# Layer 1's cross-attention on one Trainium2 core: value products turned round, on column quarters, with the sums of the weights from a second such product

## The chip, the cores and the metric

The kernel runs on one core of one Trainium2 chip. The core has five engines that the text names as the profile does: TensorE (PE, with its loads of the stationary operand as PEld), VectorE (DVE), ScalarE (ACT), GpSimd (POOL) and SyncE (SP). TensorE writes its products to PSUM[...]; POOL does not touch PSUM here. The metric is the device time of one execution in microseconds, as the median of several runs.

## The reference

A decoder of two layers works on x of 2 x 1024 tokens with 256 features, with a context of 2 x 64 tokens. Each layer has self-attention, cross-attention to the context and a feed-forward part, each followed by a layer norm. All of it is float32. The part that the change concerns is layer 1's cross-attention, with 16 heads of 16 features over 64 keys:

```python
qh = (q @ wq.T).reshape(bs, sq, N_HEADS, D_K).transpose(0, 2, 1, 3)
kh = (k @ wk.T).reshape(bs, sk, N_HEADS, D_K).transpose(0, 2, 1, 3)
vh = (v @ wv.T).reshape(bs, sk, N_HEADS, D_K).transpose(0, 2, 1, 3)
z = jnp.einsum('bhqd,bhkd->bhqk', qh, kh) / math.sqrt(D_K)
z = jnp.where(mask[:, None, :, :], jnp.float32(-10000000000.0), z)
z = jax.nn.softmax(z, axis=-1)
z = jnp.einsum('bhqk,bhkd->bhqd', z, vh)
z = z.transpose(0, 2, 1, 3).reshape(bs, sq, D_MODEL)
return z @ wo.T
```

The result is added to x and normalised; x then goes to the quantised feed-forward part, which needs the largest absolute value over all tokens before it can start.

## The kernel before, in words

The kernel is written as stages, one for each part of each layer. Layer 1's cross-attention is `l1_xattn` (L1528); it follows `l1_attn` and precedes `l1_ffn`. The 2048 tokens are cut into NT = 16 tiles of 128 tokens, and four tiles make a group (NG = 4 groups of GT = 512 tokens). The small helper functions of `l1_xattn` each issue one step for one tile:

- `queries(g)` (L1552) makes the transposed queries of a group, two PSUM banks of 512 columns; one bank is copied out by DVE, one by ACT.
- `softmax(n)` makes the scores of all 16 heads for 128 tokens in two 512-column products (L1567, against a block-diagonal form of the keys, into the tile `wide`), copies those that the mask keeps over a tile set to -1e10 (DVE, L1571, onto POOL's memset of L1564), takes the maxima (DVE, L1576), subtracts them (POOL, L1577) and takes the exponential (ACT, L1578).
- `turn(n)` transposes the weights by pairs of heads, so that the 2 x 64 keys of a pair lie on the 128 partitions (eight transposes, L1588), and copies the two halves out of PSUM, one by ACT (L74 in `evac`) and one by DVE (L70).
- `mix(n)` multiplies: the turned weights are the stationary operand, and `vblk`, which holds the values of the pair's two heads, each with a column of ones, is the moving operand (L1603). The output has tokens on partitions, and for each head 16 sums of values and one sum of weights. DVE takes the reciprocals of the 16 sums of weights (L1608) and multiplies (L1610) into `lxtok`.
- `back(n)` transposes `lxtok` by two 128x128 transposes (L1620), and ACT copies the result to `lxtokT`.
- `output(n)` multiplies by the output weights (L1634), adds the residual on DVE (L1637), and, after the third and fourth tile of a group, normalises (`normalise`, L178 to L200, with a power on POOL at L183) and takes the largest absolute value (L1644).

`vblk` is filled earlier, in `prepare` (L1447 on), whose steps are issued during layer 0's feed-forward part.

The order of the work is set in two ways. TensorE's order is written out by hand: the loop at the end of `l1_xattn` stands in a `manual_schedule` for that engine, and issues in turn the scores two tiles ahead, this tile's transposes, the output of three tiles ago, the transposes back of two tiles ago and the products of one tile ago:

```python
for n in range(NT + 3):
    ...
    softmax(n + 2)
    if n < NT:
        turn(n)
    output(n - 3)
    back(n - 2)
    mix(n - 1)
```

The orders of VectorE, ScalarE and POOL within the stage are chosen when the kernel is built, by a scheduler[...]. PSUM is shared out as two tiles `wide` of two banks, three single banks (`bank`, used by queries, turn, back and output in turn) and one accumulator (`acc`, used by `mix` alone): the products of a tile can start only when DVE has read those of the tile before.

Of the kernel before, what the change touches and what calls it, by code (L numbers as in the profile page):

```python
# [9 lines left out]
F32 = mybir.dt.float32  # L10
# [5 lines left out]
ALU = mybir.AluOpType  # L16
AX = mybir.AxisListType

P = 128
B, S, D = 2, 1024, 256  # L20
# [13 lines left out]
class Decoder:  # L34
# [11 lines left out]
    def pool(self, name, bufs, **kw):  # L46

        return self.tc.tile_pool(name=name, bufs=bufs, reuse_waits="tile", **kw)
# [1339 lines left out]
    def prepare(self, tmp):  # L1388
        nc, t, late = self.nc, self.t, self.late
        H = 16  # L1390
# [14 lines left out]
        for name in ("wq", "wo", "wk", "wv"):  # L1405
            w = tmp.tile([P, 2, D], F32, tag="lxw", name="lxw")
            nc.sync.dma_start(w, t["L1_xattn_" + name].rearrange("(o p) d -> p o d", p=P))
            ps = self.bank()
            for d in range(2):
                for o in range(2):  # L1410
                    k = 2 * d + o
# [10 lines left out]
        ps = self.bank()  # L1422
        for m in range(2):
            for c in range(2):
                nc.tensor.matmul(
                    ps[:, m * P : (m + 1) * P], lhsT=wT["wk"][:, c, m * P : (m + 1) * P],
                    rhs=self.ctxT[:, c, :], start=c == 0, stop=c == 1,
# [11 lines left out]
        ps = self.bank()  # L1439
        for b in range(B):  # L1440
            for c in range(2):
                nc.tensor.matmul(
                    ps[:, b * D : (b + 1) * D],
                    lhsT=twice[:, c, b].rearrange("p a k -> p (a k)"), rhs=wT["wv"][:, c, :],
                    start=c == 0, stop=c == 1,
                )
        self.vblk = late.tile([P, B, 8, 2, 17], F32, name="vblk")  # L1447
        nc.gpsimd.memset(self.vblk, 0.0)
        for k in range(2):
            rows = slice(k * SK, (k + 1) * SK)  # L1450
            nc.gpsimd.memset(self.vblk[rows, :, :, k, 16:17], 1.0)
            for b in range(B):
                nc.vector.tensor_copy(
                    self.vblk[rows, b, :, k, 0:16],
                    ps[rows, b * D : (b + 1) * D].rearrange("p (m k i) -> p m k i", k=2, i=16)[:, :, k, :],
                )
        yield
# [22 lines left out]
        for name in ("w_gate", "w_up"):  # L1480
            w = self.weight(None, NI, D)
# [16 lines left out]
        w = self.weight(None, 2, self.I)  # L1498
# [8 lines left out]
        for c in range(NI):  # L1507
            n = P if c < NI - 1 else last
# [6 lines left out]
        ps = self.bank()  # L1515
# [12 lines left out]
    def l1_xattn(self):  # L1528
        nc = self.nc
        H, NT = 16, T // P  # L1530
# [10 lines left out]
        with ExitStack() as s:  # L1541
            pool = lambda n, k: s.enter_context(self.pool(n, k))
            qp, pp, ptp, op = pool("lxq", 2), pool("lxp", 4), pool("lxpT", 3), pool("lxo", 3)
            qT, prob, turned, tok, tokT, res, new = {}, {}, {}, {}, {}, {}, {}
            wide = [P, H, SK]

            def queries(g):
# [33 lines left out]
            def turn(n):  # L1581
                p = prob.pop(n)
                turned[n] = ptp.tile([P, 8, P], F32, tag="lxpT", name="lxpT")
                for half in range(2):
                    ps = self.bank()
                    for k in range(4):
                        m = half * 4 + k
                        nc.tensor.transpose(  # L1588
                            ps[:, k * P : (k + 1) * P],
                            p[:, 2 * m : 2 * m + 2, :].rearrange("p h k -> p (h k)"), self.ident,  # L1590
                        )
                    self.evac(
                        turned[n][:, half * 4 : half * 4 + 4, :], ps.rearrange("p (k q) -> p k q", q=P),
                        by=nc.vector if half else nc.scalar,
                    )

            def mix(n):

                if not 0 <= n < NT:
                    return  # L1600
                ps = self.acc()[:, 0 : H * 17].rearrange("p (h i) -> p h i", i=17)
                for m in range(8):
                    nc.tensor.matmul(  # L1603
                        ps[:, 2 * m : 2 * m + 2, :], lhsT=turned[n][:, m, :],
                        rhs=self.vblk[:, n // 8, m].rearrange("p a i -> p (a i)"), start=True, stop=True,
                    )
                rz = self.sm.tile([P, H], F32, tag="lxrz", name="lxrz")
                nc.vector.reciprocal(rz, ps[:, :, 16])  # L1608
                tok[n] = op.tile([P, D], F32, tag="lxtok", name="lxtok")
                nc.vector.tensor_tensor(  # L1610
                    tok[n].rearrange("p (h i) -> p h i", i=16), ps[:, :, 0:16],
                    rz.unsqueeze(2).to_broadcast([P, H, 16]), ALU.mult,
                )

            def back(n):
                if not 0 <= n < NT:
                    return
                ps = self.bank()
                for c in range(2):
                    nc.tensor.transpose(  # L1620
                        ps[:, c * P : (c + 1) * P], tok[n][:, c * P : (c + 1) * P], self.ident
                    )
                tokT[n] = op.tile([P, 2, P], F32, tag="lxtokT", name="lxtokT")
                self.evac(tokT[n].rearrange("p c q -> p (c q)"), ps[:, 0:D], by=nc.scalar)

            def output(n):
                if not 0 <= n < NT:
                    return
                g, i = divmod(n, 4)
                if i == 0:  # L1630
                    res[g] = self.rp.tile([P, 4, D], F32, tag="r", name="r")
                ps = self.bank()[:, 0:D]
                for c in range(2):
                    nc.tensor.matmul(  # L1634
                        ps, lhsT=tokT[n][:, c, :], rhs=self.lxwoT[:, c, :], start=c == 0, stop=c == 1
                    )
                nc.vector.tensor_tensor(res[g][:, i, :], ps, self.x[g][:, i, :], ALU.add)  # L1637
                if i == 2:
                    new[g] = self.xp.tile([P, 4, D], F32, tag="x", name="xg")
                tiles = {2: range(3), 3: range(3, 4)}.get(i)  # L1640
                if tiles:
                    self.normalise(new[g], res[g], tiles)
                    k = 2 * g + i - 2
                    nc.vector.tensor_reduce(  # L1644
                        self.xm[:, k : k + 1], new[g][:, tiles.start : tiles.stop, :], AX.XY, ALU.max,
                        apply_absolute_value=True,
                    )
                if i == 3:
                    self.x[g] = new[g]

            with self.tc.manual_schedule(engines={mybir.EngineType.PE}):
                queries(0)
                softmax(0)
                softmax(1)
                for n in range(NT + 3):
                    if n < 4:
                        self.ends[n]()
                    if n % 4 == 1 and n // 4 + 1 < NG:
                        queries(n // 4 + 1)
                    softmax(n + 2)  # L1660
                    if n < NT:
                        turn(n)
                    output(n - 3)
                    back(n - 2)
                    mix(n - 1)


# [173 lines left out]
```

## Time and profile before

| What | Before |
|---|---|
| Median of 3 runs | 2464.19 us (2464.09 to 2467.39) |
| The profiled execution | 2464.71 us |
| Its span in the trace | 2462.9 us |
| PE busy over the span | 2331.8 us (95%) |
| DVE / ACT / POOL busy | 1677.5 / 1110.8 / 911.3 us |
| Layer 1's cross-attention, first scores to last maximum | 2254 to 2369.6 us |

The span is the time from the first to the last instruction of the program in the trace; the execution is 1.8 us longer. "Busy" is the time in which an engine has at least one instruction running. Matmuls overlap in the records, and their ends are modelled, so the start of one matmul to the start of the next tells more than the length of one. A float32 product or its weight load stands in the trace as two records. L numbers are lines of the kernel; L70 and L74 are the copies in the helper `evac`, and are told apart by the tile that they write. In a group's row the columns are: line, engine, operation, output and input with shapes, the count, then the busy time and the mean of one in ns, then the idle time before them with what ended it.

### The profile page before, as it was taken

What the parts mean: (1) busy time and instruction counts of PE and PEld (TensorE: products, weight loads), DVE (VectorE), ACT (ScalarE), POOL (GpSimd) and SP (SyncE); (2) the same over time, 40 slices, a digit from 0 to 9 for tenths busy, and PEclk for the clock granted to TensorE, in tenths of its full rate; (3) what the DMA queues carried; (4) which work ended last, traced back from release to release, by engine and by line L of the source; (5) the groups of instructions that cost most, each with busy time, mean ns of one, the idle gap of its engine ahead of it and who ended that gap; (6) DMA issues with size and microseconds to landing.
All of it is one profiled execution on the core that took longest, in us unless ns stands there. A gap on an engine that the chain in (4) does not pass through costs nothing. (4 is left out here: it accounts for less than half of the span.)

```text
span 2462.9 us, 37293 instructions
## 1 busy us (share of the span) xinstructions
PE 2331.8 (95%) x14062; PEld 1580.2 (64%) x14065; DVE 1677.5 (68%) x2916; ACT 1110.8 (45%) x1730; POOL 911.3 (37%) x747
## 2 busy tenths in 40 slices
PE   7999999999998999999999999999989999999974
PEld 3545545444545668899999999999734444444742
DVE  6888887888785334555555555545788687885786
ACT  4665565565563322233333333333156555664344
POOL 4666666566565222342343332332210001002412
PEclk9999999999999999999999999999999999999986
DMA  7888788688787001010010010100212121210001
GB/s 160 174 159 169 148 169 166 131 161 170 151 172 187 1 1 41 1 39 27 13 35 30 18 41 6 48 1 1 49 25 42 28 40 30 47 23 1 1 1 35
DMA packets 275667, 168.78 MB, mean 69 GB/s; under 512 B 47560, under 2 KB 262176, under 8 KB 275488
## 3 DMA queue, kind: packets, MB, share of 16 engines
q1 hardware_dynamic: 239072, 148.05, 28.6%
q10 hardware_dynamic: 36416, 18.36, 3.7%
q8 instruction: 111, 1.82, 0.3%
q14 instruction: 68, 0.56, 0.1%
HBM read 34.21 MB, written 2.10 MB: 15 GB/s over the span
## 5 line engine op out<-in xcount | busy, mean ns | idle before, releaser
L312 DVE TENSOR_REDUCE nm<-wide 128x1 f32<-128x1024 f32 x256 | 300.7, 1214 | 63.2 <-PE wide L297 62.3
L1186 DVE TENSOR_REDUCE most<-bank 128x1 f32<-128x512 f32 x476 | 300.4, 684 | 25.3 <-PE bank L1176 17.3
L1229 ACT ACTIVATE w<-wide 128x1024 f32<-128x1024 f32 x256 | 248.3, 1022 | 147.0 <-PE wide L1223 138.8
L297 PE MATMUL wide<-k,q 64*128 64x512 f32 x1024 | 271.5, 627 | 18.8 <-ACT p L317 17.4
L328 POOL TENSOR_SCALAR p<-p,sums 128x1024 f32<-128x1024 f32 x128 | 143.6, 1121 | 269.6 <-DVE sums L325 269.6
L379 PE MATMUL acc<-turned,v 128*64 128x256 f32 x2048 | 235.1, 382 | 2.2 <-ACT aoT L74 1.7
L379 PEld LDWEIGHTS acc<-turned,v 128*64 128x64 f32 x2048 | 142.6, 137 | 113.6 <-issue 30.7
L906 ACT ACTIVATE mhT<-mhT,cols 128x256 f32<-128x256 f32 (+1 forms) x256 | 143.3, 607 | 147.4 <-DVE mhT L934 105.0
L317 ACT ACTIVATE p<-wide,nm 128x1024 f32<-128x1024 f32 x128 | 142.8, 1116 | 144.9 <-DVE nm L312 118.2
L817 POOL TENSOR_TENSOR hs<-hs,mhT 128x1024 f32<-128x1024 f32 x31 | 102.5, 3307 | 241.6 <-DVE hs L815 241.6
L342 DVE STREAM_TRANSPOSE blocks<-p 128x1024 f32<-128x1024 f32 x128 | 158.0, 1234 | 43.0 <-DMA turned<-blocks 13.3
L297 PEld LDWEIGHTS wide<-k,q 64*128 64x128 f32 x1024 | 89.9, 187 | 146.1 <-issue 76.5
L183 POOL TENSOR_TENSOR rstd<-ve,nhalf 128x4 f32<-128x4 f32 (+2 forms) x28 | 26.1, 934 | 424.7 <-DVE ve L181 424.3
L917 PE MATMUL unit<-xT,w 128*128 128x256 f32 x768 | 182.3, 380 | 0.0
L974 DVE SCALAR_TENSOR_TENSOR r<-acc,gates,r 128x128 f32<-128x128 f32 x256 | 77.7, 345 | 140.4 <-PE acc L965 140.4
L342 DVE STREAM_TRANSPOSE blocks<-r 128x1024 f32<-128x1024 f32 x128 | 153.8, 1202 | 0.0
L917 PEld LDWEIGHTS unit<-xT,w 128*128 128x128 f32 x768 | 140.9, 190 | 16.9 <-issue 0.3
L328 POOL TENSOR_SCALAR r<-r,sums 128x1024 f32<-128x1024 f32 x128 | 143.6, 1122 | 0.0
L317 ACT ACTIVATE r<-wide,nm 128x1024 f32<-128x1024 f32 x128 | 142.2, 1111 | 1.1 <-DVE nm L312 0.9
L1243 PE MATMUL acc<-w,v 128*32 128x512 f32 x1024 | 137.2, 608 | 0.0
L1176 PE MATMUL bank<-kst,qst 64*128 64x512 f32 x476 | 125.9, 459 | 11.8 <-DVE most L1186 11.8
L362 POOL COPY turned<-blocks 32x1024 f32<-32x1024 f32 x128 | 132.0, 1031 | 4.0 <-DVE blocks L342 0.3
(333 smaller groups left out, 4479.3 us busy)
## 6 DMA issues: line engine op xcount, KB each, us to landing
turned<-blocks SPq DMA_DIRECT2D x636, 128.0 KB, 2.8
turned<-blocks ACTq DMA_DIRECT2D x132, 128.0 KB, 3.1
w<-in_L_ffn_W SPq DMA_DIRECT2D x16, 1024.0 KB, 5.3
q<-q SPq DMA_DIRECT2D x64, 128.0 KB, 2.3
k<-k SPq DMA_DIRECT2D x32, 128.0 KB, 2.6
qst<-qh SPq DMA_DIRECT2D x48, 64.0 KB, 2.4
qst<-ql SPq DMA_DIRECT2D x48, 64.0 KB, 2.4
kst<-kh SPq DMA_DIRECT2D x48, 64.0 KB
```

What stands on the lines that cost most here:

```text
L297: nc.tensor.matmul(sc[h][:, kb, :], lhsT=q[rows, qi, at : at + P], rhs=k[rows, ki, :], start=True, stop=True,)
L312: nc.vector.tensor_reduce(nm, sc, AX.XY, ALU.max, negate=True)
L317: nc.scalar.activation(p, sc.rearrange("p a c -> p (a c)"), AF.Exp, bias=nm, accum_out=sums[:, 0, h : h + 1],)
L328: nc.gpsimd.tensor_scalar(p, p, sums[:, 1, h : h + 1], 1.0, ALU.mult, ALU.mult)
L342: nc.vector.transpose(blocks[m][:, :, h, qt, :], p.rearrange("p (j q) -> p j q", q=32))
L362: nc.gpsimd.tensor_copy(b, a)
L379: nc.tensor.matmul(av[own[h], 0:256].rearrange("p (t i q) -> p i t q", t=2, i=4), lhsT=vals[u][:, kt, own[h]], rhs=p[:, h], start=kt == 0, ...
L906: nc.scalar.activation(hT[:, f, cols], hT[:, f, cols], AF.Relu, bias=self.cols[:, col : col + 1])
L917: nc.tensor.matmul(v[:, m, :], lhsT=up[e][k][:, f : f + P], rhs=self.halves[g][k], start=k in (1, 2, 5) and m == 0, stop=True, skip_group_ ...
L1186: nc.vector.tensor_reduce(most[n][:, kb, qt, h : h + 1], sc[a], AX.X, ALU.max, negate=True)
L1229: nc.scalar.activation(slot[:, k, :], ps[k].rearrange("p a q -> p (a q)"), AF.Exp, scale=0.25)
L1243: nc.tensor.matmul(mixed[n][o : o + 32, :], lhsT=vals[b][:, kt, 17 * h : 17 * h + 32], rhs=pT[:, a, :], start=kt == 0, stop=kt == 7, tile_ ...
```

## The change

The value product is turned round. The values become the stationary operand (32 columns: two heads of 16), and the turned weights (128 keys by 128 tokens) the moving one, so that the output has features on partitions and tokens along the free dimension. This is the form that `output` needs, so `back`, its two transposes and its copy are gone, and the loop has one step less in flight. Four pairs of heads go to four column quarters of the PE array (`tile_position=(0, 32 * j)`), that is to four groups of 32 partitions of the output. Two such sets of four make all 16 heads.

The sums of the weights can no longer be a 17th column of each head. They come from the same product with `vone` in place of `vblk`: ones for the keys of the one head in its 16 columns and for those of the other head in its 16. So every sum appears 16 times, once beside each feature, and the reciprocal is taken of a tile of 128 x 256 elements, where it was 128 x 16. Both copies of the turned weights are now made by ACT.

```diff
-        self.vblk = late.tile([P, B, 8, 2, 17], F32, name="vblk")
+        self.vblk = late.tile([P, B, 8, 2, 16], F32, name="vblk")
         nc.gpsimd.memset(self.vblk, 0.0)
+        self.vone = late.tile([P, 2, 16], F32, name="vone")
+        nc.gpsimd.memset(self.vone, 0.0)
         for k in range(2):
             rows = slice(k * SK, (k + 1) * SK)
-            nc.gpsimd.memset(self.vblk[rows, :, :, k, 16:17], 1.0)
+            nc.gpsimd.memset(self.vone[rows, k, :], 1.0)
             for b in range(B):
                 nc.vector.tensor_copy(
-                    self.vblk[rows, b, :, k, 0:16],
+                    self.vblk[rows, b, :, k, :],
...
                     self.evac(
                         turned[n][:, half * 4 : half * 4 + 4, :], ps.rearrange("p (k q) -> p k q", q=P),
-                        by=nc.vector if half else nc.scalar,
+                        by=nc.scalar,
                     )
...
-                ps = self.acc()[:, 0 : H * 17].rearrange("p (h i) -> p h i", i=17)
-                for m in range(8):
-                    nc.tensor.matmul(
-                        ps[:, 2 * m : 2 * m + 2, :], lhsT=turned[n][:, m, :],
-                        rhs=self.vblk[:, n // 8, m].rearrange("p a i -> p (a i)"), start=True, stop=True,
-                    )
-                rz = self.sm.tile([P, H], F32, tag="lxrz", name="lxrz")
-                nc.vector.reciprocal(rz, ps[:, :, 16])
-                tok[n] = op.tile([P, D], F32, tag="lxtok", name="lxtok")
-                nc.vector.tensor_tensor(
-                    tok[n].rearrange("p (h i) -> p h i", i=16), ps[:, :, 0:16],
-                    rz.unsqueeze(2).to_broadcast([P, H, 16]), ALU.mult,
-                )
-
-            def back(n):
-                if not 0 <= n < NT:
-                    return
-                ps = self.bank()
+                ps = self.acc().rearrange("p (a c q) -> p a c q", a=2, c=2)
                 for c in range(2):
-                    nc.tensor.transpose(
-                        ps[:, c * P : (c + 1) * P], tok[n][:, c * P : (c + 1) * P], self.ident
-                    )
+                    for a in range(2):
+                        for j in range(4):
+                            w = self.vone if a else self.vblk[:, n // 8, 4 * c + j]
+                            nc.tensor.matmul(
+                                ps[32 * j : 32 * j + 32, a, c, :], lhsT=w.rearrange("p a i -> p (a i)"),
+                                rhs=turned[n][:, 4 * c + j, :], start=True, stop=True,
+                                tile_position=(0, 32 * j),
+                            )
+                rz = op.tile([P, 2, P], F32, tag="lxrz", name="lxrz")
+                nc.vector.reciprocal(rz, ps[:, 1])
                 tokT[n] = op.tile([P, 2, P], F32, tag="lxtokT", name="lxtokT")
-                self.evac(tokT[n].rearrange("p c q -> p (c q)"), ps[:, 0:D], by=nc.scalar)
+                nc.vector.tensor_tensor(tokT[n], ps[:, 0], rz, ALU.mult)
...
-                for n in range(NT + 3):
+                for n in range(NT + 2):
...
-                    output(n - 3)
-                    back(n - 2)
+                    output(n - 2)
                     mix(n - 1)
```

More of the change, by code (lines that the diff above doesn't have):

```diff
@@ L1543, in l1_xattn @@
             qp, pp, ptp, op = pool("lxq", 2), pool("lxp", 4), pool("lxpT", 3), pool("lxo", 3)
-            qT, prob, turned, tok, tokT, res, new = {}, {}, {}, {}, {}, {}, {}
+            qT, prob, turned, tokT, res, new = {}, {}, {}, {}, {}, {}
             wide = [P, H, SK]
```

## The prediction

> **What bounds the kernel now.** First the page's busy times, then the table of stages, then the chain of waits inside the stage that changes.
>
> ```profile
> PE 2331.8 (95%) x14062; PEld 1580.2 (64%) x14065; DVE 1677.5 (68%) x2916; ACT 1110.8 (45%) x1730; POOL 911.3 (37%) x747
> ```
> TensorE (PE) has work throughout. The stage, layer 1's cross-attention, runs from about 2254 to 2369.6 us. The table of stages (length, then busy us of each engine, then the granted PE clock) for four of its tiles, and for the end from tile 12's value products:
> ```profile
> core 0: us, PE busy (x) PEld busy (x) DVE busy (x) ACT busy (x) POOL busy (x), PEclk, DMA share, GB/s
> 2289.87:2316.07 26.20, 25.81 (x146) 18.77 (x145) 19.90 (x40) 8.21 (x13) 12.73 (x11) 1.00 0.00 1
> 2347.92:2369.60 21.68, 15.05 (x108) 12.67 (x107) 15.98 (x49) 4.09 (x8) 4.97 (x8) 0.92 0.00 0
> ```
> Four tiles take 26.2 us, of which PE is busy 25.8 and VectorE (DVE) 19.9: DVE has 6.3 us to spare. The chain of waits through one tile lies wholly on PE:
> ```profile
> 2284.24 0.22 PE bank L1620 x2
> 2284.46 1.71 PE acc L1603 x16
> 2286.17 1.80 PE wide L1567 x4
> 2287.97 0.87 PE bank L1588 x8
> 2288.84 0.87 PE bank L1634 x4
> 2289.71 0.33 PE bank L1620 x2
> 2290.03 1.71 PE acc L1603 x16
> ```
> L1603 is the value product that is turned round, L1620 the transposes back that go. Single records step 0.1115 us, so sixteen occupy 1.78. The DVE group table gives the price of a reciprocal by row length (last field but one: mean ns):
> ```profile
> L620 DVE RECIPROCAL rs<-sum 128x4 f32<-128x4 f32 x4 | 0.7, 178 | 0.1
> L802 DVE RECIPROCAL esum<-esum 128x8 f32<-128x8 f32 x2 | 0.4, 203 | 0.1
> L1608 DVE RECIPROCAL lxrz<-acc 128x16 f32<-128x16 f32 x16 | 4.0, 251 | 4.2 <-PE acc L1603 4.2
> ```
> 178, 203, 251 ns at 4, 8, 16 elements: about 6.2 ns per element over 153 ns. And two views on the new product's kind, column quarters in layer 1's self-attention (timeline), and the clock (stages of 3.41 us):
> ```profile
> 2000.42 1.06 PE L1243 MATMUL acc<-w,v 128*32 128x512 f32 x8
> 2001.42 0.51 PE L1176 MATMUL bank<-kst,qst 64*128 64x512 f32 x2
> ```
> ```profile
> 2362.80:2366.22 3.42, 1.23 (x5) 0.68 (x4) 2.28 (x8) 0.37 (x1) 1.09 (x4) 1.00 0.00 0
> 2366.22:2369.63 3.41, 0.00 (x0) 0.00 (x0) 2.53 (x8) 0.00 (x0) 0.56 (x1) 0.50 0.00 0
> 2403.76:2407.18 3.42, 1.86 (x8) 0.77 (x8) 3.31 (x7) 2.06 (x3) 0.00 (x0) 1.00 0.00 0
> 2407.18:2410.59 3.41, 2.70 (x12) 1.11 (x11) 3.31 (x6) 1.38 (x2) 0.00 (x0) 1.00 0.00 0
> ```
> After a window in which PE was busy 1.23 us the clock is halved; after one with 1.86 us it is not.
>
> [...] four 512-column products in quarters end in 1.00 us until the next product, beside 0.86 for a single full-width one (1.72 for two at L1567). [...]
>
> **The change, part by part**, per tile of 128 tokens, 16 tiles.
> (1) Products: 8 of 1.78 us together become 16 in four rounds of four quarters. Each float32 product of 128 columns streams a quarter of 0.86 = 0.214 us; four rounds 0.86, [...] 0.14 after (1.00 - 0.86) and 0.10 before, by single records. I take 1.10. Bounds: 0.86 [...], 2.0 (weight loads of 106 ns not hidden in such short rounds), 3.4 (no overlap of quarters). PE gains 0.68.
> (2) The transposes back (0.22 on PE) and their copy on ScalarE (370 ns) go: PE gains 0.22. ScalarE has room (8.2 of 26.2 us busy), so this is worth 0.22 at most.
> (3) The second half of the weights' copy moves from DVE (680 ns, queue time 0.59) to ScalarE (0.58): two copies in a row there. The product that reads them is issued a whole tile later, which hides the second, so PE pays nothing; without that cover it would be 0.6 a tile. DVE's gain is counted in its sum below.
> (4) The reciprocal grows from 16 to 256 elements a partition: 153 + 256 x 6.25 = 1.75 us against 0.25; queue time 1.66 against 0.17. Bounds: 0.41 us, the rate of the division's multiply at L1610 (128x256, 407 ns)[...]. I take 1.75 since three rows lie on that line. The multiply keeps its size.
> (5) Setup: one more memset on POOL in the layer before (37% busy), no DMA moves, SP's queue is the same: nothing. If POOL were late there, tens of ns.
>
> PE per four tiles: 4 x (1.72 + 0.87 + 0.86 + 1.10) + 3.43 for the queries = 21.6 us instead of 25.2 (observed 26.2 with waits). DVE in queue time (start to start) per tile: masked copy 1.21, maximum 1.12, reciprocal 1.66, multiply 0.32, residual 0.33, statistics 0.39 = 5.03; per four with layer norm, maxima and a query copy (3.4) 23.5, where today's own sum gives 19.9. DVE also waits: twice for POOL's power (0.8 each in this trace) and about 0.8 on its own results: 25.9. **DVE becomes the bound, and the middle gains only 0.3 per four tiles, 1 us over twelve.** PE then waits: its output product needs the multiply, and in 6 of 16 tiles the issue order of the changed kernel puts a masked copy (1.21) between reciprocal and multiply. There product end to multiply end is 0.26 + 1.66 + 1.21 + 0.45 = 3.6 us, over PE's 2.6 us of scores and transposes; PE's queue stands behind the output product.
>
> The end, from tile 12's products: without scores to cover them, tiles run serially. Tile 12 to 13: DVE first works off layer norm, a maximum and a residual (about 5.9 us to tile 12's multiply), so 6.4; 13 to 14 and 14 to 15: 1.10 + 0.26 + 1.75 + 0.45 + 0.12 + 0.86 = 4.5, taken as 4.8 and 4.6 with the queue; tile 15 to the last maximum 8.6. Sum 24.4 against 21.7: +2.7.
>
> New: PE now idles 2 to 3.6 us at a time in this end (no gap over 0.7 us there today), so a clock window gets little work and the clock halves. On the path from tile 13 on: three products (0.85 more each) and four outputs (0.86 more each), 6.0 if all; I take 5.0.
>
> Sum: -1.0 + 2.7 + 5.0 = +6.7 on the profiled execution's 2464.71 (span 2462.9 and 1.8 around it), which is 0.5 above the median 2464.19. Rounded: **2470.5 us**.
>
> **Rivals.**
> The end keeps its clock (window edges fall well, or 1.2 us of products is enough): +1.7, 2466. For: the threshold lies somewhere from 1.23 to 1.86 us of work in a window. Against: one stall of 3.5 us fills a window.
> Faster: the reciprocal's price per element falls on long rows. Place: DVE between product and multiply. At 0.41 us DVE needs 18.2 us per four tiles, PE bounds again: up to 3 x (22.6 - 26.2) = -11, less the waits left, so -8: 2456. It decides below about 1.2 to 1.5 us. Against: the line through three row lengths; for: no row here is longer than 16.
> Dearer pieces: weight loads bare (2.0 us a tile)[...]: +9 to +17, 2477. For: rounds of 0.107 us are as long as a load's 106 ns. Against: quarters load beside each other, eight loads in 0.05 us at L1243.
> The quarters do not run side by side (the change does not do what it says): 16 x (3.4 - 1.1), PE the bound, about +33: 2497. Against: L1243.
>
> **Numbers.** Forecast 0.42, clock kept 0.25, cheaper reciprocal 0.15, dearer pieces 0.13, no overlap 0.05. A measurement tells 0.2%, 4.9 us, from no change. Slower: 0.39 of the forecast, 0.13, 0.05: 0.57. Same: most of "clock kept" and edges: 0.29. Faster: 0.14. The range 2459 to 2480 leaves out most of the cheap reciprocal (0.10), no overlap (0.05) and the dearest end (0.03). The likeliest case alone: 2468 to 2474.
>
> **What would show it.** Right: the reciprocal's row at 1.75 us x16; DVE busy near 23.5 of about 26 us per four tiles; PE idle before the output product, released by the multiply; a halved clock around the last four tiles; products near 1.1 us a tile. Wrong: a reciprocal well below 1.4 us, PE still without idle time, or products over 1.8 us.

## The result, and the profile after

The changed kernel takes 2476.76 us (median of 6 runs, 2473.67 to 2477.72); the kernel before takes 2467.39 us beside it (2464.09 to 2469.83). The ratio is 1.003, with a 95% interval of 1.0019 to 1.0041 (the two medians alone give 1.0038). Run again later beside another set of runs of before, the same two kernels gave 1.0018 (1.0009 to 1.0027). The change makes the kernel slower by 0.2 to 0.3%. The profiled execution of the changed kernel took 2477.1 us, with a span of 2475.3 us.

The first two views are the busy times of the page and the table of stages of the changed kernel. The stages are two groups of four tiles in the middle, and the end from tile 12's products to the last maximum.

```profile
PE 2333.7 (94%) x14289; PEld 1569.3 (63%) x14289; DVE 1693.0 (68%) x2900; ACT 1112.8 (45%) x1730; POOL 910.6 (37%) x748
```
```profile
core 0: us, PE busy (x) PEld busy (x) DVE busy (x) ACT busy (x) POOL busy (x), PEclk, DMA share, GB/s
2306.25:2332.80 26.55, 22.88 (x201) 13.90 (x200) 25.43 (x39) 8.90 (x13) 12.77 (x11) 1.00 0.01 1
2332.80:2355.70 22.90, 19.73 (x196) 12.43 (x196) 21.51 (x34) 8.19 (x12) 11.17 (x9) 1.00 0.00 1
2355.70:2382.71 27.01, 14.31 (x161) 9.72 (x160) 19.62 (x38) 3.19 (x5) 4.11 (x7) 0.74 0.00 1
```

The page's busy shares hardly differ; the table of stages shows what changed. VectorE is now busy for 25.43 of 26.55 us and for 21.51 of 22.90 us, where it had over 6 us to spare in four tiles. PE, which was nearly full, now has over 3 us to spare in each group. The end takes 27.0 us, where it took 21.8, at a granted clock of 0.74.

The groups of the stage, by shape (mean ns in the last field but one):

```profile
L1615 DVE RECIPROCAL lxrz<-acc 128x256 f32<-128x256 f32 x16 | 27.9, 1745 | 1.2 <-PE acc L1609 1.2
L1617 DVE TENSOR_TENSOR lxtokT<-acc,lxrz 128x256 f32<-128x256 f32 x16 | 6.5, 408 | 0.1
```

The long reciprocal takes 1745 ns. Next, PE's order in three tiles of the middle (timeline), and all of PE's larger waits from the first value products to the last maximum (line waiting, what it waits for, total us, times, longest):

```profile
2338.96 0.43 PE L1609 MATMUL acc<-lxpT,vblk 128*32 128x128 f32 x8
...
2339.97 1.98 PE L1569 MATMUL wide<-w,lxqT 128*128 128x512 f32 x4
2341.80 1.04 PE L1590 MATMUL bank<-ident,lxp 128*128 128x128 f32 x8
2342.82 1.13 PE L1627 MATMUL bank<-lxwoT,lxtokT 128*128 128x256 f32 x4
2343.88 0.43 PE L1609 MATMUL acc<-lxpT,vblk 128*32 128x128 f32 x8
...
2344.89 1.98 PE L1569 MATMUL wide<-w,lxqT 128*128 128x512 f32 x4
2346.71 1.04 PE L1590 MATMUL bank<-ident,lxp 128*128 128x128 f32 x8
2348.72 1.13 PE L1627 MATMUL bank<-lxwoT,lxtokT 128*128 128x256 f32 x4 [0.98 <-DVE lxtokT L1617]
2349.78 0.43 PE L1609 MATMUL acc<-lxpT,vblk 128*32 128x128 f32 x8
```
```profile
PE bank L1627 <- DVE lxtokT L1617: 14.6, 10, 3.1
PE bank L1627 <- DVE mv L179: 3.3, 1, 3.3
```

The sixteen quarter products of a tile lie between 2338.96 and 2339.97: 1.01 us. One tile, from 2338.96 to 2343.88, takes 4.92 us, with no wait that the view marks. The next takes 5.90 us: PE waits 0.98 us at the output product, for VectorE's multiply, and everything behind it in PE's queue waits too (the next tile's products start at 2349.78). Why the multiply is late there can be read from VectorE's order in this tile:

```profile
2345.46 1.75 DVE L1615 RECIPROCAL lxrz<-acc 128x256 f32<-128x256 f32 x1
2347.12 1.24 DVE L1573 COPY_PREDICATED lxp<-keep,wide 128x1024 f32<-128x1024 uint8 x1
2348.26 0.41 DVE L1617 TENSOR_TENSOR lxtokT<-acc,lxrz 128x256 f32<-128x256 f32 x1
```

A masked copy of a later tile's scores stands between the reciprocal and the multiply. Of the 16 tiles, six have it there, tiles 0, 5, 6, 8, 10 and 11, all in the first twelve. PE waits for the multiply in every one of the six, 7.4 us together, and only once elsewhere among the first twelve (tile 4, 0.65 us). In the kernel before, over the same part, PE waited for that multiply only twice, 1.6 us in all, at the transposes back.

For the comparisons below, the stage is measured at the same points in every kernel. "Middle" is from the start of tile 0's value products to the start of tile 12's, "end" from there to the last maximum, and "stage" is the sum. The last column begins earlier, at the first score product (one expectation below calls it the first query product, which starts 3.5 us before it), since some kernels below do more work ahead of tile 0's products.

| Kernel | Middle, us | End, us | Stage, us | From first score product, us | Ratio (95%) |
|---|---|---|---|---|---|
| before | 75.5 | 21.8 | 97.3 | 115.4 | 1 |
| changed | 74.2 | 27.0 | 101.2 | 119.5 | 1.003 (1.0019 to 1.0041) |
| changed, again | 75.8 | 26.6 | 102.4 | 120.6 | 1.0018 (1.0009 to 1.0027) |
| changed, copy for reciprocal | 63.8 | 21.8 | 85.6 | 103.9 | 0.9947 (0.9934 to 0.9961) |
| changed, half the copies on VectorE | 80.4 | 27.4 | 107.9 | 126.1 | 1.0045 (1.003 to 1.006) |
| before, both copies on ScalarE | 73.0 | 21.3 | 94.4 | 112.5 | 0.9995 (0.9985 to 1.0005) |
| changed, PE kept busy at the end | 74.2 | 25.1 | 99.4 | 117.6 | 1.0016 (1.0006 to 1.0025) |
| changed, old form in the last four tiles | 75.4 | 22.4 | 97.8 | 116.0 | 0.9993 (0.9982 to 1.0005) |
| changed, scaling and query copy on ScalarE | 76.3 | 24.0 | 100.3 | 118.5 | 1.0007 (0.9997 to 1.0016) |
| changed, VectorE's order by hand | 89.3 | 31.0 | 120.3 | 138.6 | 1.0092 (1.0076 to 1.0108) |
| divide before turning | 78.2 | 18.0 | 96.2 | 126.3 | 1.0025 (1.0014 to 1.0035) |
| the same, one maximum a token | 66.7 | 15.9 | 82.6 | 108.7 | 0.9965 (0.995 to 0.9979) |
| the same, scaling and query copy on ScalarE | 60.6 | 16.0 | 76.6 | 101.9 | 0.9947 (0.9932 to 0.9961) |
| changed, one maximum a token | 74.5 | 27.6 | 102.1 | 118.7 | 0.9999 (0.9988 to 1.0011) |

The stage explains 3.9 us (5.1 in the second profile) of the 12.4 us between the two profiled spans. The larger part, 9.2 us, was there before the stage began, where the two programs do the same work but for a memset. The profiles give no sign that it is an effect of the change: in eight profiles of the new form with the same lead-in, the first value products start between 2269.4 and 2281.5 us. The two profiles of the one changed kernel start them at 2281.5 and 2278.5 us; before starts them at 2272.3 us, and before with both copies on ScalarE at 2277.3 us. The timed ratios, 1.003 and 1.0018, are 7.4 and 4.4 us of 2464. The 4.4 fits what the stage lost; the 7.4 is larger, and its interval begins at 4.7 us, above the 3.9 of the first profile and below the 5.1 of the second.

### The profile page after: what moved, and what is told of

Same layout as the page of the kernel before. It is cut to its first block, busy times and chain, and to the rows that moved or that the text cites. A ratio compares the mean times of both kernels' runs of the same rounds, so it can differ in the third digit from the quotient of the medians.

```text
span 2475.3 us, 37702 instructions
## 1 busy us (share of the span) xinstructions
PE 2333.7 (94%) x14289; PEld 1569.3 (63%) x14289; DVE 1693.0 (68%) x2900; ACT 1112.8 (45%) x1730; POOL 910.6 (37%) x748
## 3 DMA queue, kind: packets, MB, share of 16 engines
q1 hardware_dynamic: 239072, 148.05, 28.6%
```

## The experiments

**Is it the reciprocal?** In the changed kernel its place is taken by a plain copy of the same shape, which has a row of 408 ns (it leaves the division out).

```diff
-                nc.vector.reciprocal(rz, ps[:, 1])
+                nc.vector.tensor_copy(rz, ps[:, 1])
```

> The changed kernel with the reciprocal of the 128x256 sums replaced by a plain copy of the same size (the division is left out: tokens are multiplied by the sums). Theory A (VectorE is the bound because the reciprocal costs 1.75 us a tile): the row falls to about 0.41 us, PE bounds the middle again, first products to the 13th from 74.2 to about 67 us, the end from 27.0 to about 21, the whole about 12 us below the changed kernel and 4 to 8 below the one before. Theory B (the quarter products[...] on PE are the bound, VectorE only looks busy): the stage stays within 2 us of 101.2. Theory C (the loss lies before the stage, not in it): also no change of the stage beyond what the copy saves, and the first products still start at about 2281 us where the kernel before has 2272.

Measured: 2455.83 us, ratio 0.9947; the stage falls from 101.2 to 85.6 us, 11.7 us below before. PE's waits for the multiply, in the same stretch as above, shrink from ten with 14.6 us to this:

```profile
PE bank L1627 <- DVE lxtokT L1617: 3.9, 2, 2.8
PE bank L1627 <- DVE mv L179: 3.0, 1, 3.0
```

So the change's other parts are worth a gain, and 1.34 us a tile of reciprocal turns it into a loss. PE is the bound again:

```profile
2275.42:2339.20 63.78, 63.78 (x602) 40.83 (x601) 55.51 (x103) 26.50 (x41) 36.89 (x28) 1.00 0.01 1
2298.45:2320.53 22.08, 22.08 (x201) 13.83 (x200) 19.56 (x38) 8.78 (x13) 12.78 (x11) 1.00 0.01 1
```

The first line is the whole middle, the second four of its tiles with a group of query products (only two such groups fall into the middle). They take 22.1 us, where the prediction's sum for PE was 21.6. VectorE's order changed with this build, too: no masked copy stands between the copy to `lxrz` and the multiply in any of the twelve tiles. The end is back at before's 21.8 us.

**The two copies of the turned weights.** First the changed kernel with the second copy back on VectorE, then before with both on ScalarE.

```diff
-                        by=nc.scalar,
+                        by=nc.vector if half else nc.scalar,
```

> The changed kernel with the second half of the weights' copy back on VectorE. Theory A: VectorE is the bound and gets 0.59 us more a tile, so the stage grows by 7 to 9 us (101.2 to about 109). Theory B: no change, or up to 1 us less since ScalarE no longer makes two copies in a row.

Measured: ratio 1.0045, stage 107.9 us, 5.5 and 6.7 us above the two profiles of the changed kernel and so short of the 7 to 9 expected. The middle is 4.6 to 6.2 us longer. Twelve copies of 0.59 us in VectorE's queue are 7.1 us, so most of each appears in the time.

> The kernel before with both halves of the weights' copy on ScalarE, the one part of the change that can be made alone. Theory A: VectorE had 6.3 us to spare in four tiles and ScalarE 18, so the stage stays within 1 us of 97.3. Rival: the second copy in a row delays the products; then up to 0.58 us a tile, 9 us in all.

Measured: ratio 0.9995, whose interval holds 1. The profile has the stage 2.9 us shorter, more than the 1 us either way that was allowed for. The ratio cannot tell whether that gain repeats.

**How much is chance?** The changed kernel, again.

> The changed kernel again, for the part ahead of the stage. Theory A: the stage is again 101 us within 0.5 (3.9 more than before), and the start of the stage differs between runs of one kernel by as much as it did between the two (9 us), so the start is chance. Theory C: the stage starts near 2281 us again, with every kernel that has the new form, and near 2272 with the old form.

Measured: ratio 1.0018, stage 102.4 us, start of the stage 2278.5 us. Neither theory came in as stated: the stage is 1.1 us longer, not within 0.5, and the start moved by 3.0 us, not 9. This run by itself would fit Theory C; the spread of the other profiles, above, speaks against it.

The 1.6 us by which the middle differs have a visible cause. In the traces of before and of the changed kernel the granted clock is 1.00 or 0.50, and each stretch at 0.50 that ends within the program lasts 3.41 us or a whole multiple of it (up to 20.48). Two windows of 3.41 us of this profile (length, busy us of PE, PEld, DVE, ACT, POOL, then the clock):

```profile
2312.43:2315.84 3.41, 1.28 (x7) 0.75 (x5) 3.41 (x4) 2.02 (x3) 1.79 (x2) 1.00 0.00 0
2315.84:2319.26 3.42, 3.42 (x35) 2.24 (x35) 2.57 (x6) 1.06 (x1) 1.90 (x1) 0.50 0.00 0
```

PE's wait of 2.13 us for tile 5's multiply lies within one window here, and the next window, full of work, runs at half clock; tile 6 then takes 7.37 us. In the first profile the same wait falls across the edge of two windows, with 1.81 and 2.89 us of PE's work, the clock stays at 1.00, and tile 6 takes 5.82 us. So the change has a cost in the middle that comes and goes: the middle is 74.2, 74.2 and 74.5 us in the profiles of the new form with the changed kernel's order that keep the full clock there, and 75.8 and 75.4 in those with one halved window. A difference of that size between two single profiles can be this alone.

**The clock at the end.** In the changed kernel, PE is given six 512-column bfloat16 products, which no one reads, in each of the last steps of the loop.

```diff
                     if n < NT:
                         turn(n)
+                    if n >= NT - 2:
+                        ps = self.wide()[:, 0, :]
+                        for _ in range(6):
+                            nc.tensor.matmul(
+                                ps, lhsT=self.identb, rhs=self.wdT[:, 0:2, :].rearrange("p a d -> p (a d)"),
+                                start=True, stop=True,
+                            )
```

> The changed kernel with six idle bf16 products of 512 columns (about 1.3 us) on PE after the transposes of the last two tiles and in the two steps behind them, into a score bank that nothing reads, so that PE does not fall idle in the end. Theory A as predicted (the halved clock costs 5 us there): from the 13th products to the last maximum 27 becomes 22. Theory A with the size that the trace suggests (chain +2.7, clock +2.5): 24.5. Rival (PE waits for VectorE anyway, the halved clock is hidden): within 0.5 us of 27.

Measured: ratio 1.0016, end 25.1 us, 1.5 to 1.9 us shorter than without, nearest to the middle one of the three expectations. The timed ratio cannot show a gain of this size. The table of windows of the changed kernel's end, then of this one's (length, busy us of PE, PEld, DVE, ACT, POOL, then the clock):

```profile
2358.27:2361.68 3.41, 0.61 (x3) 0.59 (x4) 2.89 (x7) 1.53 (x2) 1.51 (x2) 1.00 0.00 0
2361.68:2365.09 3.41, 3.41 (x39) 2.28 (x38) 2.41 (x6) 0.00 (x0) 0.22 (x1) 0.50 0.03 7
2365.09:2368.51 3.42, 2.46 (x38) 1.84 (x40) 2.13 (x4) 1.07 (x2) 0.00 (x0) 1.00 0.00 0
2368.51:2371.92 3.41, 0.98 (x19) 0.69 (x8) 2.57 (x4) 0.00 (x0) 0.00 (x0) 1.00 0.00 0
2371.92:2375.33 3.41, 2.68 (x35) 1.49 (x33) 1.86 (x5) 0.00 (x0) 1.08 (x4) 0.50 0.00 0
2375.33:2378.75 3.42, 1.06 (x3) 0.88 (x4) 3.17 (x6) 0.00 (x0) 0.00 (x0) 0.50 0.00 0
```
```profile
2346.31:2349.72 3.41, 1.42 (x7) 0.77 (x6) 2.91 (x7) 1.53 (x2) 1.52 (x2) 1.00 0.00 0
2349.72:2353.13 3.41, 3.41 (x39) 2.29 (x38) 2.37 (x6) 0.00 (x0) 0.24 (x1) 0.50 0.03 7
2353.13:2356.55 3.42, 3.42 (x40) 2.38 (x42) 2.08 (x4) 1.07 (x2) 0.00 (x0) 1.00 0.00 0
2356.55:2359.96 3.41, 2.38 (x27) 1.19 (x18) 2.66 (x4) 0.00 (x0) 0.00 (x0) 1.00 0.00 0
2359.96:2363.38 3.42, 2.98 (x41) 1.48 (x39) 2.71 (x5) 0.00 (x0) 1.08 (x4) 1.00 0.00 0
```

In the changed kernel the windows with 0.61 and 0.98 us of PE's work are each followed by a halved one. Between them the clock is full again, after a halved window that was full of work. With the filler the second fall comes only at 2366.79, 2.1 us before the end, when PE's part of the stage is done. The first remains, although its window now has 1.42 us of work. By an estimate from its clock of 0.50, the halved window that remains can have cost up to half of its 3.41 us, 1.7 us. If the filler itself cost nothing, the clock's part of the end is then 1.5 us at least and 3.6 us at most. The last two steps of this end, from tile 14's products to tile 15's and from there to the last maximum, take 4.54 and 8.41 us, where the prediction had 4.6 and 8.6 without the clock and the changed kernel took 4.88 and 10.04.

**The old form where nothing covers the new one.** The last four tiles use the old product, transposes back and short reciprocal; the first twelve use the new form (`OLD` is 12).

```diff
+                if n >= OLD:
+                    return old_mix(n)
...
-                    output(n - 2)
+                    if n - 2 < OLD:
+                        output(n - 2)
+                    if n - 3 >= OLD:
+                        output(n - 3)
+                    back(n - 2)
                     mix(n - 1)
```

> The changed kernel whose last four tiles are mixed in the old form (tokens on partitions, a reciprocal of 128x16, transposes back); tiles 0 to 11 stay in the new form. Theory A: the middle stays at 74 to 76 us, the end falls from 27 to about 22, the stage is 96 to 98 as in the kernel before (97.3), so the whole equals the kernel before within 0.1%. Rival (the end is slow for another reason than the new form): the end stays near 27.

Measured: ratio 0.9993, no difference from before; the end is 22.4 us, close to before's 21.8. So the loss of the changed kernel lies in the end. The middle of 75.4 us has a halved window like that above, at 2312.64, and equals before's 75.5; without one the new form is 1.0 to 1.3 us shorter than before over the twelve tiles.

**VectorE's sum, or the loop through it?** In the changed kernel, layer norm's scaling and the copy of the queries go to ScalarE. In the changed kernel's middle these operations took VectorE 5.3 us (ten scalings, two copies); a small operation for each normalisation, 0.7 us together, is new.

```diff
-                    self.normalise(new[g], res[g], tiles)
+                    self.normalise(new[g], res[g], tiles, nc.scalar)
...
-                    self.evac(qT[g][:, m, :], ps, 0.25)
+                    self.evac(qT[g][:, m, :], ps, 0.25, by=nc.scalar)
```

> The changed kernel with the scaling of the layer norm (1.4 us per four tiles, with its waits for POOL) and the second query copy (0.6) moved from VectorE to ScalarE. Theory A (VectorE's queue is the bound of the middle): 2.0 us of work less and up to 1.6 of waits, at 0.1 more for one small operation: 12 tiles 74 -> 64 to 69 us, the end 27 -> 25 to 27, the stage about 92 to 95, below the kernel before by 2 to 5. Theory B (PE waits in its own queue are the bound): within 1 us of 101.

Measured: ratio 1.0007; the middle is 76.3 us, with one halved window, and not shorter than the 75.8 of the profile that has one too, where 4.6 us would show. The end is 24.0 us, 2.6 to 3.0 us shorter, in part because VectorE had a maximum more behind it when the end began; the whole stage is 1.0 to 2.1 us shorter. VectorE's waits in the stage (same columns as PE's above):

```profile
DVE r L1630 <- PE bank L1627: 5.6, 5, 2.2
DVE off L191 <- POOL rstd L183: 3.4, 5, 1.0
DVE lxp L1573 <- PE wide L1569: 2.3, 5, 1.1
DVE xm L1637 <- ACT xg L196: 2.1, 3, 1.2
```

Much of the time that VectorE saved came back as waits, for PE's output and scores and for ScalarE's scaled rows. What sets the middle's pace is thus not VectorE's sum alone. A reading that fits these runs is a loop: the work of one tile runs round through two engines: products 1.01, hop 0.14, from the reciprocal's start to the multiply's 1.79, from there to the output product 0.58 (all in tile 14, from 2367.78), then 1.06 to the next tile's products (in tile 9), since the output stands ahead of them in PE's queue. That is 4.6 us. Where a masked copy stands between, as in six of the first twelve tiles, the 1.79 is 2.80 (in tile 10), and the sum 5.6. In this reading, work taken out of the loop counts (the reciprocal), and work beside it counts less. The copies put back on VectorE above stand beside the loop, and most of their time showed, so the sum counts too.

The loop is argued and not isolated, and this run is no clean test of it. The order of VectorE's queue is chosen anew for each build, and here the masked copy stands between reciprocal and multiply in seven of the twelve tiles, one more than before; tile 9, which had no wait, has one of 1.10 us now. PE's wait for the multiply in the middle is 8.9 us, where it was 8.1. That the order, and not the loop as such, ate the gain is a rival that no run here excludes.

**VectorE's order by hand.** The manual schedule is extended to VectorE, so that its queue follows the order in which the code issues the steps.

```diff
-            with self.tc.manual_schedule(engines={mybir.EngineType.PE}):
+            with self.tc.manual_schedule(engines={mybir.EngineType.PE, mybir.EngineType.DVE}):
```

> The changed kernel with VectorE's order by hand as the program has it: the multiply follows its reciprocal at once, and no masked copy comes between. Theory A (the sum of VectorE's work bounds, the order counts little): stage within 3 us of 101, with PE's waits for the multiply shorter and VectorE's waits for POOL longer. Rival (the copy placed between reciprocal and multiply is the cost, 1.2 us in six tiles): stage 94 or less.

Measured: ratio 1.0092, stage 120.3 us, far outside the 3 us either way that were allowed for. PE then waits for the multiply up to 4.8 us at a time (19.5 us in seven waits), and VectorE waits bare for layer norm's power on POOL. This order changes much more than the one masked copy, so what that copy costs is not separated here: no copy stands between now, and PE waits longer than before, for other reasons.

**Another place for the division.** The weights are divided before they are turned, where a tile has only 128 x 16 sums. The second product, the long reciprocal and the multiply go. The scores are issued three tiles ahead instead of two.

```diff
                 nc.scalar.activation(p, p, AF.Exp)
+                sums = self.sm.tile([P, 2, H], F32, tag="lxsum", name="lxsum")
+                nc.vector.tensor_reduce(sums[:, 0], p, AX.X, ALU.add)
+                nc.vector.reciprocal(sums[:, 1], sums[:, 0])
+                nc.gpsimd.tensor_tensor(p, p, sums[:, 1].unsqueeze(2).to_broadcast(wide), ALU.mult)
...
-                rz = op.tile([P, 2, P], F32, tag="lxrz", name="lxrz")
-                nc.vector.reciprocal(rz, ps[:, 1])
                 tokT[n] = op.tile([P, 2, P], F32, tag="lxtokT", name="lxtokT")
-                nc.vector.tensor_tensor(tokT[n], ps[:, 0], rz, ALU.mult)
+                self.evac(tokT[n], ps[:, 0], by=nc.scalar)
...
-                    softmax(n + 2)
+                    softmax(n + 3)
```

> Same result by another order: the weights are divided before they are turned, where tokens lie on partitions and a tile has 128x16 sums. After Exp, VectorE adds each head's 64 weights (a pass like the maximum, 1.12 us), takes 128x16 reciprocals (0.17), and GpSimd multiplies (1.9 us, as its subtraction). The products of the sums, the long reciprocal and the multiply go; ScalarE copies the product to SBUF (0.37). Scores are issued three tiles ahead, not two. Start from the stage of 101.2 us in the changed kernel, 97.3 before. Theory (the loop from product over reciprocal to output product holds PE): it is cut to 0.5 + 0.3 + 0.4 + 0.1 + 0.9, so PE's own work, 4 x (1.72 + 0.87 + 0.86 + 0.55) + 3.43 = 19.4 us per four tiles, or VectorE's, 23.5 - 4 x 0.69 = 20.8, sets the pace: 21 to 23 us, stage 85 to 91, ratio 0.994 to 0.998. Rival, VectorE's sum with its 2.4 us of waits was the bound: 23.2 us per four tiles, stage 92 to 94, ratio 0.998 to 1.000. Second rival, GpSimd with 20.3 us of work per four tiles and a chain of some 10 us from scores to turned weights becomes the bound: stage above 96, not faster than before.

Measured: ratio 1.0025, stage 96.2 us, and 126.3 us from the first score product: the second rival. The long chain of the softmax is what is late, as ScalarE's largest wait in the middle shows:

```profile
ACT lxp L1580 <- POOL lxp L1579: 27.4, 11, 5.1
```

The exponentials wait for POOL's subtraction, which now shares POOL with a second pass of 1.9 us a tile. POOL is busy for 53 of the middle's 78 us, so the length of the chain through it is a likelier cost than its sum. Over three quarters of the middle the granted clock is 0.88 and 0.89, in stretches where PE is busy for 24.5 of 28.6 and 24.4 of 30.6 us. The end, which has no long reciprocal, is short: 18.0 us.

**POOL's subtraction taken away.** One maximum over all heads of a token goes to Exp as its bias.

```diff
-                nm = self.sm.tile([P, H], F32, tag="lxnm", name="lxnm")
-                nc.vector.tensor_reduce(nm, p, AX.X, ALU.max, negate=True)
-                nc.gpsimd.tensor_tensor(p, p, nm.unsqueeze(2).to_broadcast(wide), ALU.add)
-                nc.scalar.activation(p, p, AF.Exp)
+                nm = self.sm.tile([P, 1], F32, tag="lxnm", name="lxnm")
+                nc.vector.tensor_reduce(nm, p, AX.XY, ALU.max, negate=True)
+                nc.scalar.activation(p, p, AF.Exp, bias=nm)
```

> The kernel that divides before turning, with one more edit: one maximum over all 16 heads of a token instead of one a head, given to Exp as its bias, so that GpSimd's subtraction (1.9 us a tile) goes; the result is the same wherever no head's scores lie far below the token's largest, and here they lie within 6.4. If GpSimd or the length of the chain from scores to turned weights bounds the kernel that divides first, this gains up to 1.9 us a tile, 4 to 7 us per four tiles, and brings the stage to 84 to 90. If PE or VectorE bounds it (20.8 us per four tiles of VectorE unchanged), the middle stays within 2 us of that kernel's and only the chain ahead of the last tiles could gain, 0 to 2 us. If waits of VectorE for GpSimd's results cost it 0.5 us a tile, the gain lies between, some 6 us over the stage.

Measured: ratio 0.9965, faster than before; stage 82.6 us, a little below the 84 to 90 that were expected if POOL bounds. From the first score product it is 17.6 us less than with the subtraction. The last eight tiles of its middle, in two windows, and PE's largest single wait there:

```profile
2303.30:2330.20 26.90, 21.17 (x137) 12.06 (x136) 24.42 (x40) 10.52 (x17) 13.56 (x12) 1.00 0.00 1
2330.20:2348.70 18.50, 16.28 (x129) 9.94 (x128) 18.25 (x29) 9.45 (x16) 7.13 (x7) 1.00 0.00 1
```
```profile
PE wide L1569 <- DVE lxqT L72: 3.2, 1, 3.2
```

In the second window VectorE is busy nearly all the time. In the first, PE stands for 3.2 us before a score product, since VectorE's half of the query copy is late in VectorE's queue. The edit shortens the chain and takes work off POOL at once; which of the two bought the time stays open.

**Now relieve VectorE.** The two moves to ScalarE that bought nothing measurable in the changed kernel's middle, on top of this one. Beside it on the same chip ran the changed kernel with only the one maximum a token.

> The kernel with one maximum a token that divides before turning (108.7 us from the first query product to the last maximum, VectorE busy 18.25 of 18.5 us in four of its tiles), and both layer norm's scaling and the queries' copies on ScalarE. The same two moves gained nothing in the changed kernel (stage 100.3 beside 101.2 to 102.4 us). Theory: there the loop over the reciprocal was the bound and here it is VectorE's sum, so here they do gain: 4 x 0.3 + 0.6 = 1.8 us of VectorE's queue time per four tiles, 3 to 6 us over the stage up to where PE's 19.4 us per four tiles or the start bounds it: 102 to 106, ratio 0.994 to 0.996. Rival: these moves buy nothing anywhere, since the maxima and statistics then wait for ScalarE (1.2 us each time, as in the changed kernel with them): 108 to 110, ratio as without them, 0.9965.

Measured: 2455.79 us, ratio 0.9947; 101.9 us from the first score product, 6.8 less than without the moves (the two timed intervals still overlap, from 0.995 to 0.9961). In this form the moves count. They count in two ways that this run does not part: VectorE's busy time in the middle falls from 60.9 to 56.3 us, and PE's wait of 3.2 us for the query copy is gone, since ScalarE makes that copy. So of the 6.8 us at most 3.6 are left for VectorE's sum as the bound. This kernel is faster than before by 13.1 us by its ratio. Tiles 4 to 7 of its middle:

```profile
2306.46:2328.41 21.95, 21.00 (x139) 12.00 (x138) 20.48 (x34) 13.92 (x24) 12.16 (x10) 1.00 0.00 1
```

PE is busy for 21.00 of 21.95 us and VectorE for 20.48. PE's own sum for this form had been put at 19.4 us, and little is left to gain without less work on both.

> The changed kernel with one maximum a token as Exp's bias, so that GpSimd's subtraction (1.9 us a tile) goes; products of the sums, long reciprocal and multiply stay. Theory (the loop product, reciprocal, multiply, output product sets the pace, GpSimd is not in it): middle within 2 us of 74.2 to 75.8, end 0 to 2 us shorter than 26.6 to 27.0, stage 98 to 103, ratio 1.000 to 1.003; what gained 16 us between the two kernels that divide first was then GpSimd's second pass there, and not the maximum by itself. Rival: scores that arrive too late are a part of the changed kernel's waits, so 1.9 us less in their chain brings the stage to 90 to 96 and the ratio below 0.999.

Measured: middle 74.5, end 27.6, stage 102.1 us, as the loop predicts; ratio 0.9999. POOL's subtraction does not set the changed kernel's pace, and PE's wait for the multiply is still there:

```profile
PE bank L1626 <- DVE lxtokT L1616: 15.3, 10, 3.2
```

The ratio is at the low edge of what was expected, and its upper bound, 1.0011, still allows 2.7 us of loss where the stage shows 4.8. From the first score product the loss is 3.3 us, since tile 0's products come 1.6 us sooner after it.

## Why the prediction was right

The forecast was 2470.5 us, from a sum of +6.7 us (which on the median of 2464.19 gives 2470.9). The stage lost 3.9 and 5.1 us in two profiles, and the timed ratios are 4.4 and 7.4 us. The sign, the rough size and the main costs hold. The separate steps do not all hold, and that the 7.4 us lie closer to the forecast than what the stage lost is luck.

- **Reciprocal, 1.75 us expected: right.** 1745 ns. The line through rows of 4, 8 and 16 elements carries to 256: from 16 to 256 elements the measured slope is 6.2 ns an element.
- **Quarter products, 1.10 us: right, 0.09 too high.** 1.01 us. That is below the 2.0 us that bare weight loads and the 3.4 us that quarters one after another would have taken by the prediction's estimates, so the rivals "dearer pieces" and "no overlap" fall. Of the 1.01, 0.86 is the estimate for four rounds, each a quarter of the 0.86 us that a 512-column product takes; what the other 0.15 consists of no run here isolates.
- **The middle, -1.0 us: right in size where the clock stays full, in part right in reason.** Measured -1.3 with the full clock and +0.3 with one halved window. The prediction put nothing down for the clock in the middle, though a halved window follows one of the very waits that it forecast there. VectorE's sum came out as expected: 25.43 and 21.51 us in two groups, mean 23.47, where 23.5 was predicted. But "VectorE becomes the bound" as a sum is too simple: taking 4.6 us off it in the middle did not shorten the middle. PE's wait at the output product is where the time goes. The prediction had this wait as a side remark beside the sum, with the masked copy between reciprocal and multiply in 6 of 16 tiles; it is six, and they hold 7.4 of the 8.1 us that PE waits for the multiply there. Whether the sum, the loop or this order sets the pace stays open.
- **Transposes back and their copy, the second copy on ScalarE: near what was costed.** With the reciprocal replaced, PE's sum of 21.6 us per four tiles is nearly reached (22.1). Moving one copy back costs 4.6 to 6.2 us in the middle, where its twelve turns in VectorE's queue are 7.1. The setup has no run of its own.
- **The end, +2.7 of chain and +5.0 of clock: the clock term is the step that was mis-sized.** The end grew by 5.2 and 4.8 us, not 7.7. What it forecast is there: PE waits for 3.28 us before its output product at 2361.07, and in the window from 2361.68 the granted clock is 0.50. In that window tile 13's products take 1.87 us (2362.45 to 2364.32), 0.86 more than the 1.01 at full clock. But the prediction let every product and output from tile 13 on run at half clock. In the trace the clock came back in between, after a halved window with 3.41 us of work. Ahead of the stage there is a full window after which it did not, as the last section shows. The clock's part is 1.5 to 3.6 us, by the filler and the halved window that it left; the chain's is then 1.6 to 3.3 us (5.2 less 1.9 to 3.6, or 4.8 less 1.5 to 3.2), around the 2.7 expected. How it divides within that stays open. The prediction's bracket for the clock, a threshold between 1.23 and 1.86 us of PE's work in a window, does not hold either: its own trace breaks it, as the last section shows.
- **The rival "cheaper reciprocal"** gave 2456 us for a reciprocal of 0.41; with a copy of 0.41 us in its place the kernel took 2455.83. That agreement is luck: before ran at 2469.86 us beside it, so the gain was 13.1 us by the ratio and 11.7 in the stage, where the rival had 8. Its premise was wrong, but it named the right term: the reciprocal's row decided the sign.
- **What the forecast did not know:** the profiled execution alone was 12.4 us above before's, and three quarters of that lies ahead of the stage, within what the other profiles show as chance. Judged by that single execution, the forecast would have seemed 6.6 us short. By the stage its +6.7 is 1.6 to 2.8 us too high; the two timed ratios lie on either side of it.

## What to carry to other kernels

Before a reduction is turned into a form in which its result is replicated, multiply the price per element of what is then done with it by the new row length: here a reciprocal at 6.2 ns an element, 16 times longer, ate a real gain on PE. When a second engine comes close to full, ask whether its sum, or the place of single operations in its queue, makes the first engine wait, because taking work off it does not always buy time: the same two moves to ScalarE gained nothing measurable in the middle of one form, and 6.8 us in the other, where one of the moved operations had held PE for 3.2 us by itself. Do the division where the row is short, but count the length of the chain it joins: it paid only once another pass of that chain was gone.

## What the runs showed of the hardware

PE's busy time in a window of 3.41 us does not by itself tell whether the next window runs at half clock. In the stage, windows with 0.61, 0.98, 1.28 and 1.42 us are followed by a halved one. But in the trace of before, ahead of the stage, one with 1.56 us is followed by full clock, and ones with 2.22 and even 3.21 us are followed by half clock:

```profile
768.78:772.19 3.41, 1.56 (x6) 1.06 (x6) 0.23 (x1) 0.00 (x0) 2.34 (x1) 1.00 0.77 142
772.19:775.60 3.41, 2.22 (x10) 1.69 (x11) 0.42 (x1) 2.68 (x4) 0.00 (x0) 1.00 0.72 134
792.67:796.09 3.42, 2.22 (x9) 0.93 (x7) 1.79 (x5) 0.41 (x1) 1.37 (x4) 1.00 1.04 389
796.09:799.50 3.41, 3.41 (x5) 1.48 (x5) 0.69 (x1) 1.46 (x2) 3.33 (x4) 0.50 0.24 76
1017.95:1021.37 3.42, 3.21 (x15) 2.12 (x13) 2.58 (x5) 0.78 (x2) 3.34 (x2) 1.00 0.00 0
1021.37:1024.78 3.41, 3.41 (x9) 2.47 (x8) 1.38 (x2) 0.00 (x0) 1.23 (x1) 0.50 0.00 0
1024.78:1028.19 3.41, 3.41 (x15) 2.76 (x15) 0.69 (x1) 0.00 (x0) 0.00 (x0) 0.50 0.00 0
```

Nor does a full window always bring the clock back: in the stage a window at half clock with 3.41 us of work was followed by full clock and one with 2.68 us was not, but the window at 1021.37 is full and is followed by another halved one. What else counts, no run here shows. GpSimd's pass over 128 x 1024 elements takes 1.90 us for a subtraction and for a multiplication alike, against 1.2 us for VectorE's maximum or sum over the same tile.
